# A planned issue order learns of the SBUF port shared by VectorE and GpSimd, and takes its durations from the trace

## The chip, the cores and the metric

The kernel runs on one core of a Trainium2 chip, in one launch. The metric is device time in microseconds (us). The engines are named as the profile names them: PE is the matmul engine (TensorE), PEld its weight loads, DVE is VectorE, ACT is ScalarE, POOL is GpSimd, and SP is the engine whose queue issues every DMA of this kernel. All five take their instructions in program order; one that waits holds up everything behind it on its engine.

## The reference, cut to what matters

The input is 64 sequences of 64 tokens with 256 features, with a context of the same shape. Six pre-norm layers are added one after the other to a residual `x`:

```python
x = x + _L0_attn_ref(_layernorm(x), ...)
x = x + _L0_xattn_ref(_layernorm(x), ctx_2048, ctx_2048)
x = x + _L0_ffn_ref(_layernorm(x), ...)
x = x + _L1_attn_ref(_layernorm(x), ...)
x = x + _L1_xattn_ref(_layernorm(x), ctx_2048, ...)
x = x + _L1_ffn_ref(_layernorm(x), ...)
```

In the kernel they are called a0, x0, f0, a1, x1 and f1. The layer a0 is a causal attention with 16 query heads and 4 key heads of 128, normalised queries and keys and a rotation (RoPE). The layer x0 is an attention over features with 8 heads of 8 tokens each: every head has a 256 by 256 table of scores. The layer f0 is a linear layer plus a routed low-rank expert. The layer a1 is a causal attention with 16 query heads of 16 and one key head. The layer x1 is a cross-attention with 16 heads of 128; only the first 257 context positions are used, which here is the whole context of a sequence. The layer f1 is a gated feed-forward with 704 inner features, whose activations and weights are rounded to 8-bit steps.

## The kernel before

**Tiling.** The 4096 tokens are cut into 16 groups of 256 (`GT`), a residual tile `xt` of 128 partitions by 2 by 256 for each. The first half of the program takes every group through a0, x0, f0 and a1 and stores the residual in DRAM (`mid`); the second half loads it again and does x1 and f1. The halves overlap a little: the first groups of x1 begin while the last groups of the first half run. Set-up work (splitting weights into a high and a low fp16 part, Gram matrices, rounding the f1 weights) is spread between them.

**The planner.** Nothing is emitted where the layer code stands. The layer functions only record operations: `s.o(engine, cost, reads, writes, fn)`, or `s.alt([...], reads, writes)` where two or three engines could do it. `Sched.plan` (L245) then simulates the program greedily with the given costs in ns: at each step it computes for every ready operation the earliest start (ends of what it depends on plus a hand-over time from the table `LATS`, a free buffer, and the time at which its engine is free), sorts the candidates by start, due time and cost, and takes the first that cannot deadlock the buffer pools. `PEN = 400` is added to a DVE candidate that has an alternative. Due times come from `PACE`, `SHIFT` and the table `LEAD` (L1777 on), some 130 offsets by layer and tile. `pe_run` (L225) models PE's clock in windows of `TICK`. `Sched.emit` (L354) calls the recorded functions in the order of the planned starts. The times of the plan are then forgotten: on the chip every engine runs its list in order and waits on semaphores. The only things that the plan decides are the order of each engine's list, the engine of each `alt`, and the assignment of buffers.

**Costs.** `c_act`, `c_acts`, `c_dve`, `c_dve2` and `c_pool` (L363 to L380) give the cost of an operation from its number of elements; many small ones are written as numbers. The plan before knows no dependence between DVE and POOL other than through data.

**Names that the prediction's steps touch.**
- `phl` (L604 to L608, in `softmax_rows`): the normalised probabilities, split into a high part (ACT) and a low part (POOL, or DVE as the alternative). A transposing DMA (`dma_T`, L526) then makes `pt` or `pT`, the input of the PV matmuls (`po` L641, `ctx` L1283, `pc_ps` L1489).
- `xhl` (L540 to L543, in `to_T`): the same split of the normalised residual, then transposed into `xT`. `q1hl` (L1241 to L1244) is the same for a1's queries.
- `ku`, `qu` (L784 to L789, in `rope_bank`): the rotated keys and queries of a0. POOL multiplies (L787), POOL or DVE adds (L788, L789).
- `ln_mv`, `ln_rs`, `xh` (L512 to L521): layer norm. DVE computes statistics, POOL the power, DVE the scaling (`xh` L521).
- `xs_ps` (L990): x0's scores, a pair of matmuls into one PSUM bank, of which DVE takes the row maxima (`xmx` L996). There are 512 pairs. `xt_ps` (L1025): the transposed scores, again 512 pairs, of which ACT takes the exponential (`xpt` L1031). The PSUM pool has 8 banks (`COUNTS`, class B), shared by everything.
- `fam`, `fsc`, `f_w`, `f_b` (L1643 to L1647 and L1619) and `fs` (L1660): the rounding of f1's weights in five chunks on DVE, and the store of the scales to DRAM, one for `w_gu` and one for `w_dn`. It happens at the change-over, when the x0 of the last group is done.
- `acc` of x1 (L387 to L389, by `n_proj`): 48 matmuls for each half of a group's tokens and each block of heads.

Of the kernel before, what the change touches and what calls it, by code (L numbers as in the profile page):

```python
# [13 lines left out]
AF = mybir.ActivationFunctionType  # L14
ALU = mybir.AluOpType
# [6 lines left out]
GT = 256  # L22
# [53 lines left out]
class Sched:  # L76
# [168 lines left out]
    def plan(self):  # L245
        self.clock = [0, 0.0, False]
        free = {e: 0.0 for e in self.ENG}
        slots = {c: [0.0] * n for c, n in self.counts.items()}
# [20 lines left out]
        while ready:  # L269
# [5 lines left out]
            for o in ready:  # L275
                if o.grp > lim and o.grp == int(o.grp):
                    continue
                est = o.tmin
                if o.prev:
                    est = max(est, o.prev[0].start + o.prev[1])  # L280
                for d in o.deps:
                    est = max(est, d.end + LATS[d.eng][o.alts[0][0]])
                need = {}
                for t in o.new:
                    if not t.held:
                        need.setdefault(t.cls, []).append(t)
                ok = True
                for c, n in need.items():
                    fr = slots[c]
                    if len(fr) < len(n):  # L290
                        ok = False
                        break
                    est = max(est, fr[len(n) - 1])
                if not ok:
                    continue
                for e, c, fn in o.alts:
                    st = max(est, free[e])
                    for t in o.new:
                        if t.bank:
                            for e2, u in t.bank.items():  # L300
                                if e2 != e and u + LAT > st:
                                    st = u + LAT
                    cands.append((st, o.due, o.idx, st + c, o, e, fn, need))
                    if st < first[e]:
                        first[e] = st
# [13 lines left out]
            st, _, _, end, o, e, fn, _ = best  # L319
# [42 lines left out]

def c_act(n, ap=0):  # L363
    return 60 + 0.834 * n + 93 * ap


def c_acts(n):
    return 93 + 0.834 * n


def c_dve(n, ap=0):
    return 66 + 1.042 * n + 63 * ap


def c_dve2(n, ap=0):
    return 66 + 0.53 * n + 60 * ap
# [28 lines left out]
def pow2_scale(e, am, exp2, name, root=True):  # L405
# [10 lines left out]
    s.o("PE", 240, [am], [ps], lambda a, p: nc.tensor.matmul(  # L416
# [33 lines left out]
def split_weight(e, src, kc, n, dst, name, prep=None):  # L450
# [30 lines left out]
    for i, w in enumerate(ws):  # L481
# [15 lines left out]
        s.o("DVE", c_dve(pw, 1), [w, sc, hs], [ls], lambda t, a, b0, b, hv=hv, lv=lv:  # L497
# [7 lines left out]
def layer_norm(e, xt, scale=XS):  # L505

    nc, s = e.nc, e.s
    mv = s.T("sm", [128, 2, 2], name="ln_mv")
    st = s.T("sm", [128, 2, 6], name="ln_st")

    for j in range(2):
        s.o("DVE", 336, [xt], [st.sub(j)], lambda x, t, j=j: nc.vector.bn_stats(t[:, j, :], x[:, j, :]))  # L512
    for j in range(2):
        s.o("DVE", 76, [st.sub(j)], [mv.sub(j)], lambda t, m, j=j: nc.vector.bn_aggr(m[:, j, :], t[:, j, :]))
    s.o("DVE", 70, [], [mv], lambda m: nc.vector.tensor_scalar(  # L515
        m[:, :, 1], m[:, :, 1], 1e-5, scale ** -2.0, ALU.add, ALU.mult))
    rs = s.T("sm", [128, 2], name="ln_rs")
    s.o("POOL", 650, [mv], [rs], lambda m, r: nc.gpsimd.tensor_tensor(r, m[:, :, 1], e.mhalf, ALU.pow))  # L518
    xh = s.T("k2", [128, 2, D], name="xh")
    for j in range(2):  # L520
        s.o("DVE", c_dve2(D, 2), [xt, mv, rs], [xh.sub(j)], lambda x, m, r, h, j=j: nc.vector.tensor_scalar(  # L521
            h[:, j, :], x[:, j, :], m[:, j, 0:1], r[:, j:j + 1], ALU.subtract, ALU.mult))
    return xh
# [10 lines left out]
def to_T(e, xh):  # L534
# [8 lines left out]
           ("DVE", c_dve(512), lambda x, _, h: nc.vector.tensor_tensor(h[:, :, 1], x, h[:, :, 0], ALU.subtract))],  # L543
# [26 lines left out]
def softmax_rows(e, s1, scale, fold=False, planes=False):  # L570
# [10 lines left out]
    elif planes:  # L581
        s.o("ACT", 1040, [scale], [s1], lambda a, t: nc.scalar.activation(t, t, AF.Exp, scale=a))
    else:
# [4 lines left out]
        s.o("ACT", 2 * 613, [scale], [s1], f)  # L588
# [7 lines left out]
    s.o("DVE", 165, [], [sm], lambda m: nc.vector.reciprocal(m, m))  # L596
    s.o("DVE", 82, [], [sm], lambda m: nc.vector.tensor_scalar(m, m, 4096.0, None, ALU.mult))
    hls = []
    pl = (lambda t, a: t[:, a]) if planes else (lambda t, a: t[:, :, a])
    for j in range(2):  # L600
# [7 lines left out]
               ("DVE", c_dve(512), lambda t, _, p, h=h: nc.vector.tensor_tensor(pl(p, 1), t[:, h], pl(p, 0), ALU.subtract))],  # L608
# [16 lines left out]
def pv_block(e, phl, vs):  # L625
# [5 lines left out]
    for j in range(2):  # L631
        pt = s.T("k2", [128, 8, 128], F16, name="pt")
        dma_T(e, phl[j], pt, lambda t: t.rearrange("p h a l -> p (h a l)"))
        for hh in range(2):
# [8 lines left out]
            s.o("PE", 4 * 121, vs + [pt], [po], g)  # L643
# [129 lines left out]
def rope_bank(e, ps, tab, dst):  # L773
# [8 lines left out]
    for i in range(2):  # L782
        s.o("ACT", c_act(512), [ps], [sw.sub(i)],
            lambda p, w, i=i: nc.scalar.copy(w[64 * i:64 * i + 64], p[64 - 64 * i:128 - 64 * i]))  # L784
# [3 lines left out]
    s.alt([("DVE", c_dve(512), lambda w, d: nc.vector.tensor_tensor(view(d), view(d), w, ALU.add)),  # L788
# [4 lines left out]
def l0_attn(e, xt):  # L793
    nc, s = e.nc, e.s
    w = e.l0
# [3 lines left out]
    for blk in range(2):  # L799
# [10 lines left out]
        s.o("PE", 480, [sq, w.one], [ss], f)  # L810
# [13 lines left out]
        for c2 in range(4):  # L824
# [3 lines left out]
            if c2 % 2 == 1:  # L828
# [6 lines left out]
                s.o("PE", 500, [sqs[-2], sqs[-1], w.one], [ss], f, duty=0.85)  # L835
# [9 lines left out]
        s.o("PE", 220, [sss], [pst], f)  # L845
# [12 lines left out]
        s.o("PE", 440, [rb], [rk], f)  # L858
# [13 lines left out]
        s.o("PE", 540, [w.tab[0][2], kf], [bps], f, duty=0.79)  # L872
# [4 lines left out]
        for j in range(2):  # L877
# [8 lines left out]
            s.o("PE", 8 * 165, qu + [kf], [sps], f, duty=0.65)  # L886
# [43 lines left out]
def stack_rows(e, src, scale, dst, rows):  # L930
# [4 lines left out]
    if isinstance(scale, float):  # L935
        s.o("ACT", c_act(512), [src], [hl.sub(0)], lambda x, h: nc.scalar.activation(h[:, 0], x, AF.Copy, scale=scale))
        s.o("DVE", c_dve(512), [src, hl.sub(0)], [hl.sub(1)], lambda x, h0, h: nc.vector.scalar_tensor_tensor(
            h[:, 1], x, scale, h[:, 0], ALU.mult, ALU.subtract))
    else:
        s.o("ACT", c_act(512, 1), [src, scale], [hl.sub(0)],  # L940
            lambda x, a, h: nc.scalar.activation(h[:, 0], x, AF.Identity, scale=a))
        s.o("DVE", c_dve(512), [src, scale, hl.sub(0)], [hl.sub(1)], lambda x, a, h0, h: nc.vector.scalar_tensor_tensor(
# [11 lines left out]
def l0_xattn(e, xt, g, I):  # L954
# [24 lines left out]
    for j in range(2):  # L979
        mx = s.T("sm", [128, 4, 4, 2], name="xmx")  # L980
        sp = [None, SPACE[0]]
        for bs in range(4 * j, 4 * j + 4):
            for v in range(2):
                for h in range(2):
# [8 lines left out]
                    s.o("PE", 230, rows(v) + [K.sub((u, r)) for u in range(2) for r in range(3)], [ps], f, duty=0.46)  # L993
# [5 lines left out]
        s.o("PE", 110, [mx], [mps], lambda m, p: nc.tensor.transpose(p, m.rearrange("p a b c -> p (a b c)"), e.ident))  # L999
# [11 lines left out]
    for j in range(2):  # L1011
        y = s.T("k1", [128, 2, 2, 2, 4, 8], name="y")
        for b in range(2):
            po = s.T("B", [128, 2, D], name="xo_ps")
            for hs in range(2):
                bs = (2 * j + b) * 2 + hs
                pt = [s.T("k2", [128, 2, D], name="xpt") for _ in range(4)]
                for v in range(2):
                    for h in range(2):
# [8 lines left out]
                        s.o("PE", 230, rows(v) + [Q[v].sub((v, 3, j)), K], [ps], f, duty=0.46)  # L1028
# [23 lines left out]
            s.o("PE", 440, [so], [pt_], f)  # L1052
# [3 lines left out]
            s.o("DVE", 170, [pt_], [rc], lambda p, r: nc.vector.reciprocal(r, v4(p)[:, :, :, 8]))  # L1056
# [5 lines left out]
            s.o("DVE", 270, [pt_, rc], [y.sub(b)], f)  # L1062
# [5 lines left out]
        s.o("PE", 220, [y], [yo], f)  # L1068
# [19 lines left out]
def l0_ffn(e, xt):  # L1088
# [6 lines left out]
    for j in range(2):  # L1095
# [23 lines left out]
        s.o("PE", 110, [hm], [pt], lambda h, p: nc.tensor.transpose(p, h.rearrange("p a r -> p (a r)"), e.ident))  # L1119
# [3 lines left out]
        s.o("PE", 470, [hT, w.bw], [po], lambda h, b, p: nc.tensor.matmul(p, h, b, start=True, stop=True))  # L1123
# [63 lines left out]
def l1_attn(e, xt):  # L1187
# [25 lines left out]
    s.o("DVE", c_dve(GT, 1), [k1, w.hl, kh], [K],  # L1213
# [11 lines left out]
    s.o("ACT", 4 * 90, [ps], [v1], f)  # L1225
# [5 lines left out]
    s.o("DVE", 720, [v1, w.m2], [vbd], f)  # L1231
# [11 lines left out]
    s.alt([("DVE", c_dve(512), lambda x, h0, h: nc.vector.tensor_tensor(h[:, 1], x, h[:, 0], ALU.subtract)),  # L1243
# [14 lines left out]
    for j in range(2):  # L1258
# [28 lines left out]
        s.o("PE", 690, [vbd] + pTs, [cps.sub(j)], f, duty=0.46)  # L1287
# [17 lines left out]
def gram_setup(e, I, name):  # L1305
# [42 lines left out]
    s.o("DVE", c_dve(514), [g, sc, w.w.sub(0)], [w.w.sub(1)],  # L1348
# [5 lines left out]
def value_out_setup(e, I):  # L1354
# [28 lines left out]
    for b in range(4):  # L1383
        u = pieces(s, 8, 256, f"x1wn{b}")
        d = s.fixed(e.dx.tile([128, 2, 2048], F16, tag=f"wdn{b}", name="wd"))
        for i in range(4):
# [9 lines left out]
            s.o("DVE", c_dve(512, 1), [t, sc, hl.sub(0)], [hl.sub(1)], lambda t, a, h0, h:  # L1396
# [117 lines left out]
def rms_gram(e, g, T, x, xs=1.0):  # L1514
# [3 lines left out]
    for j in range(2):  # L1518
# [14 lines left out]
        s.o("DVE", 75, [ps], [ac], lambda p, ac: V.tensor_tensor(ac, ac, p[:, 256:257], ALU.add))  # L1533
# [3 lines left out]
    s.o("POOL", 740, [ms], [rs], lambda m, r: nc.gpsimd.tensor_tensor(r, m, e.mhalf, ALU.pow))  # L1537
# [3 lines left out]
def l1_xattn(e, xt, g, I):  # L1541
# [8 lines left out]
    s.o("DVE", c_dve(512, 1), [ctx, e.ctx_sc, chl.sub(0)], [chl.sub(1)], lambda x, a, _, t:  # L1550
# [16 lines left out]
    s.o("DVE", 330, [w.bo, rk], [L], f)  # L1567
# [5 lines left out]
    s.o("PE", 430, [L, w.i2], [rps], f)  # L1573
# [6 lines left out]
    for blk in range(2):  # L1580
        es = s.T("sm", [128, 2], name="x1esc")
        s.o("DVE", 130, [rq, w.exps[blk]], [es], lambda r, a, t: nc.vector.tensor_scalar(t, r, a, None, ALU.mult))
        k = [s.T("k2", [128, 2, GT], name="k8") for _ in range(4)]
        q = [s.T("k2", [128, 2, GT], name="q8") for _ in range(4)]
        for (dst, nm, T, bias) in ((k, "ki", cTs, w.kb), (q, "q", xT, w.qb)):
            for c2 in range(4):
# [10 lines left out]
                s.alt([("DVE", c_dve(512), f1), ("ACT", 716, f2)], [ps, bias], [dst[c2]])  # L1597
        s1 = s.T("k4", [128, 16, S], name="s1")
        for j in range(2):
# [9 lines left out]
            s.o("PE", 8 * 165, q + k, [sps], f, duty=0.65)  # L1609
# [59 lines left out]
def l1_ffn(e, xt):  # L1669
# [9 lines left out]
    s.o("DVE", 70, [am], [sx], lambda am, sx: V.tensor_scalar(sx, am, 1.0 / 127, 1e-8, ALU.mult, ALU.max))  # L1679
    s.o("DVE", 75, [sx], [ix], lambda sx, ix: V.reciprocal(ix, sx))  # L1680
# [8 lines left out]
    for j in range(2):  # L1689

        gu = [s.T("k4", [128, 2, HI], name="gu") for _ in range(2)]
        for a in range(4):
# [18 lines left out]
        s.o("DVE", c_dve(704), [gu[0]], [sig], lambda g, t: V.scalar_tensor_tensor(t, t, 1.0, g, ALU.add, ALU.mult))  # L1711
        s.o("DVE", c_dve(704), [sig], [ah.sub(j)], lambda t, ah, c=c: V.tensor_reduce(
            ah[:, c], t, AX.XY, ALU.max, apply_absolute_value=True))
        s.o("DVE", 75, [sx], [s2.sub(j)], lambda x, s2, c=c: V.tensor_tensor(s2[:, c], x[:, c], x[:, c], ALU.mult))
        s.chain("DVE", [
            (75, lambda s2, ah, sh, ih, c=c: V.tensor_tensor(ah[:, c], ah[:, c], s2[:, c], ALU.mult)),
            (75, lambda s2, ah, sh, ih, c=c: V.tensor_scalar(sh[:, c], ah[:, c], 1.0 / 127, 1e-8, ALU.mult, ALU.max)),
            (75, lambda s2, ah, sh, ih, c=c: V.reciprocal(ih[:, c], sh[:, c])),  # L1718
            (75, lambda s2, ah, sh, ih, c=c: V.tensor_tensor(ih[:, c], ih[:, c], s2[:, c], ALU.mult))],
# [13 lines left out]
        s.o("PE", 6 * 117, [hT, w.dn], [po], f)  # L1733
# [231 lines left out]
```

## Time and profile before

| | us |
|---|---|
| median of 3 runs | 2777.41 (2777.24 to 2780.94) |
| the profiled execution | 2781.26 |
| its span (first to last instruction) | 2779.5 |
| PE busy | 2460.3 |
| DVE busy | 2139.8 |
| ACT busy | 1521.3 |
| POOL busy | 1499.2 |
| granted TensorE clock, mean | 0.942 |

PE has over 24,000 matmuls. Its busy time contains stretches at the lower clock, in which a matmul takes twice as long. The span is longer than PE's busy time by 319 us. DVE's busy time includes what an instruction waits inside the engine once it has begun: the same operation on the same shape can have very different durations in the trace. Bytes are few (82 GB/s on average).

### The profile page before, as it was taken

Reading aid. Unit: us, or ns where it says so; the run is one execution under the profiler, and the core shown is the slowest. Engines: PE = TensorE matmul, PEld = TensorE weight load, DVE = VectorE, ACT = ScalarE, POOL = GpSimd, SP = SyncE. Lnnn points to the kernel's source line nnn. Section 1 sums busy time; section 2 is a strip of 40 time slices with the busy share of each in tenths; the row PEclk is TensorE's granted clock in tenths of the full one; section 3 lists DMA queues with packets and bytes.
Section 4 is the critical chain, followed back from the end, with each engine's and each line's share of the span. In section 5 each row is a group of like instructions: output and inputs, shape, how many; then the busy total and the mean of one; then the engine's idle time right before and its main releaser. Section 6 shows DMA issues by size and latency. Waiting matters only on the chain.

```text
span 2779.5 us, 61709 instructions
## 1 busy us (share of the span) xinstructions
PE 2460.3 (89%) x24136; PEld 1718.9 (62%) x24136; DVE 2139.8 (77%) x4827; ACT 1521.3 (55%) x2878; POOL 1499.2 (54%) x1258
## 2 busy tenths in 40 slices
PE   4889988989889989999899899579999999999995
PEld 3656565545565655565465556357777778877773
DVE  8886887898888879789888776637776767767765
ACT  6755637557568656666674466244544444444441
POOL 5895556686776768668767344223333333333321
PEclk9989999989999999999999999789999999999997
DMA  6333235345445345423345543413223232222211
GB/s 187 77 73 68 47 78 128 97 109 124 92 128 145 91 100 113 113 62 75 76 86 119 139 81 68 73 34 61 53 51 62 58 64 52 53 51 53 58 31 33
DMA packets 488532, 226.55 MB, mean 82 GB/s; under 512 B 341808, under 2 KB 463792, under 8 KB 488240
## 3 DMA queue, kind: packets, MB, share of 16 engines
q1 hardware_dynamic: 488240, 222.60, 35.5%
q8 instruction: 190, 3.11, 0.5%
q14 instruction: 102, 0.84, 0.1%
HBM read 87.98 MB, written 33.56 MB: 44 GB/s over the span
## 4 chain that ended last, share of the span: by engine, by line
PE 55%; DVE 18%; DMA 7%; ACT 4%; POOL 4%; issue 3%; SPq 1%; POOLq 0%; DVEq 0%; ACTq 0%
PE acc L387 4%; PE acc L389 4%; PE acc L388 4%; PE qk_ps L387 4%; PE xt_ps L1025 4%; PE qk_ps L389 4%; PE qk_ps L388 4%; DVE xmx L996 4%; PE pc_ps L1489 3%; PE xo_ps L1039 3%; PE xs_ps L990 2%; PE s_ps L1607 2%; DMA xT<-xhl 2%; PE s_ps L885 1%; DMA pt<-phl 1%
## 5 line engine op out<-in xcount | busy, mean ns | idle before, releaser
L1031 ACT ACTIVATE xpt<-xt_ps,xes 128x512 f32<-128x512 f32 x512 | 341.2, 689 | 113.8 <-PE xt_ps L1025 104.3
L996 DVE TENSOR_REDUCE xmx<-xs_ps 128x2 f32<-128x512 f32 x512 | 330.4, 681 | 38.1 <-PE xs_ps L990 34.5
L578 POOL TENSOR_TENSOR s<-s,sm_mx 128x1024 f32<-128x1024 f32 x96 | 184.6, 1924 | 254.0 <-DVE sm_mx L577 240.9
L389 PE MATMUL acc<-x1wn,pc 128*128 128x256 f16 x1024 | 280.9, 274 | 2.9 <-DVE pc L1495 2.9
L387 PE MATMUL acc<-x1wn,pc 128*128 128x256 f16 x1024 | 280.9, 274 | 0.5 <-ACT pc L1493 0.4
L388 PE MATMUL acc<-x1wn,pc 128*128 128x256 f16 x1024 | 280.8, 274 | 0.0
L604 POOL TENSOR_TENSOR s<-s,sm_sm 128x512 f32<-128x512 f32 x192 | 207.0, 1096 | 127.0 <-DVE f1ih L1718 73.0
L518 POOL TENSOR_TENSOR ln_rs<-ln_mv,mhalf 128x2 f32<-128x2 f32 x96 | 69.7, 726 | 340.0 <-DVE ln_mv L515 318.2
L1025 PE MATMUL xt_ps<-ovl 64*128 64x256 f16 x1024 | 197.2, 276 | 14.1 <-DMA ovl<-mneg 5.7
L990 PE MATMUL xs_ps<-ovl 64*128 64x256 f16 x1024 | 167.4, 294 | 45.8 <-DVE xmx L996 33.0
L1495 DVE SCALAR_TENSOR_TENSOR pc<-pc_ps,pc 128x512 f16<-128x512 f32 x256 | 162.8, 679 | 42.8 <-ACT pc L1493 42.3
L1596 ACT ACTIVATE q<-qk_ps,x1qb 128x256 f32<-128x256 f32 x250 | 104.8, 470 | 150.9 <-PE qk_ps L389 145.0
L607 POOL TENSOR_TENSOR phl<-s,phl 128x512 f16<-128x512 f32 x139 | 169.5, 1229 | 29.4 <-ACT phl L606 29.1
L784 ACT COPY sw<-q_ps 64x512 f32<-64x512 f32 x256 | 148.3, 580 | 61.3 <-PE q_ps L389 48.3
L787 POOL TENSOR_TENSOR sw<-sw,rp0s 128x512 f32<-128x512 f32 x128 | 167.6, 1320 | 15.1 <-ACT sq L785 14.9
L606 ACT CAST phl<-s 128x512 f16<-128x512 f32 x192 | 115.8, 618 | 104.1 <-POOL s L604 100.6
L1596 ACT ACTIVATE k<-qk_ps,x1kb 128x256 f32<-128x256 f32 x250 | 104.5, 470 | 108.8 <-PE qk_ps L389 87.5
L1493 ACT ACTIVATE pc<-pc_ps 128x512 f16<-128x512 f32 x256 | 131.6, 623 | 43.0 <-PE pc_ps L1489 42.7
L990 PEld LDWEIGHTS <-ovl 64*128 64x128 f16 x1024 | 64.9, 97 | 141.7 <-issue 126.5
L387 PE MATMUL q_ps<-xT,l0w 128*128 128x256 f16 x512 | 144.9, 283 | 6.6 <-DVE xmx L996 2.4
L789 POOL TENSOR_TENSOR qu<-qu,sw 128x512 f32<-128x512 f32 x116 | 148.3, 1286 | 3.9 <-DVE nr_t L562 2.8
L387 PE MATMUL qk_ps<-cTs,x1wki 128*128 128x256 f16 x512 | 142.6, 278 | 5.8 <-DVE pc L1495 4.0
(424 smaller groups left out, 7671.4 us busy)
## 6 DMA issues: line engine op xcount, KB each, us to landing
ovl<-hl_d SPq DMA_DIRECT2D x192, 64.0 KB
vx<-vt SPq DMA_DIRECT2D x64, 128.0 KB
ctx<-in_ctx_dram SPq DMA_DIRECT2D x32, 256.0 KB
hl_d<-hl SPq DMA_DIRECT2D x64, 128.0 KB
q1st<-q_d SPq DMA_DIRECT2D x128, 64.0 KB
wd<-w_hl SPq DMA_DIRECT2D x32, 256.0 KB
cst<-chl SPq DMA_DIRECT2D x64, 128.0 KB
xt<-in_x_dram SPq DMA_DIRECT2D x16, 256.0 KB
```

The costliest lines, as they stand in the source:

```text
L387: nc.tensor.matmul(out, lh, rh, start=(st and i == 0), stop=False, **kw)
L388: nc.tensor.matmul(out, lh, rl, start=False, stop=False, **kw)
L389: nc.tensor.matmul(out, ll, rh, start=False, stop=(i == n - 1), **kw)
L578: s.o("POOL", 1900, [mx], [s1], lambda m, t: nc.gpsimd.tensor_tensor(t, t, bc(m, 2, 64), ALU.subtract))
L604: s.o("POOL", 1030, [sm], [s1.sub(j)], lambda m, t, h=h: nc.gpsimd.tensor_tensor(t[:, h], t[:, h], bc(m[:, h], 2, 64), ALU.mult))
L607: s.alt([("POOL", c_pool(482), lambda t, _, p, h=h: nc.gpsimd.tensor_tensor(pl(p, 1), t[:, h], pl(p, 0), ALU.subtract)), ("DVE", c_dve(512 ...
L787: s.o("POOL", 1225, [sg], [sw], lambda t, w: nc.gpsimd.tensor_tensor(v(w), v(w), bc(t, 1, 8), ALU.mult))
L990: nc.tensor.matmul(a[-1][:, mc, :], q0[hh, bs, 128 * mc:128 * mc + 128], k[hh, bs, :], start=True, stop=True)
L996: nc.vector.tensor_reduce(m[:, 2 * v + h, bs % 4, :], p, AX.X, ALU.max))
L1025: nc.tensor.matmul(p[:, n, :], k[hh, bs, 128 * n:128 * n + 128], q[hh, bs, :], start=True, stop=True)
L1031: nc.scalar.activation(t, p, AF.Exp, scale=a))
L1596: nc.scalar.activation(d[:, c, :], p[:, c, :], AF.Identity, bias=b[:, b0 + c:b0 + c + 1])
```

## The change

`plan` keeps, beside the time at which each engine is free, a time for the port on DVE's side and one on POOL's side. Every POOL operation counts as using the port; a DVE operation does if its cost is of the new type `Port`, a float with a name. A POOL operation starts in the plan no earlier than the end of the last Port operation on DVE, and a Port operation on DVE no earlier than the end of the last POOL operation. The other changes are numbers: costs are set anew, most of them higher, few lower (`ctx` on PE from 690 to 510, the score matmuls from 165 to 150 each). `c_dve2`, and the new `c_dves` that replaces `c_dve` where both inputs lie in SBUF, return a `Port`. `LEAD`, `PACE`, `SHIFT`, `PEN`, `LATS` and all recorded functions stay as they are. The diff, cut to its core; the left-out lines are of the same kinds:

```diff
@@ plan
         free = {e: 0.0 for e in self.ENG}
+        port = dict(DVE=0.0, POOL=0.0)
...
                 for e, c, fn in o.alts:
                     st = max(est, free[e])
+                    if e == "POOL":
+                        st = max(st, port["DVE"])
+                    elif isinstance(c, Port):
+                        st = max(st, port["POOL"])
...
-            st, _, _, end, o, e, fn, _ = best
+            st, _, _, end, o, e, fn, _, lock = best
+            if lock or e == "POOL":
+                port[e] = end
             if e == "PE":
                 end = self.pe_run(st, end - st, o.duty)
...
+class Port(float):
+    pass
+
 def c_act(n, ap=0):
-    return 60 + 0.834 * n + 93 * ap
+    return 88 + 0.834 * n + 100 * ap
 def c_acts(n):
-    return 93 + 0.834 * n
+    return 148 + 0.834 * n
 def c_dve(n, ap=0):
-    return 66 + 1.042 * n + 63 * ap
+    return 72 + 1.042 * n + 63 * ap
+def c_dves(n, ap=0):
+    return Port(c_dve(n, ap))
 def c_dve2(n, ap=0):
-    return 66 + 0.53 * n + 60 * ap
+    return Port(66 + 0.53 * n + 60 * ap)
...
@@ layer_norm
-    s.o("DVE", 70, [], [mv], lambda m: nc.vector.tensor_scalar(
+    s.o("DVE", Port(130), [], [mv], lambda m: nc.vector.tensor_scalar(
...
-    s.o("POOL", 650, [mv], [rs], lambda m, r: nc.gpsimd.tensor_tensor(r, m[:, :, 1], e.mhalf, ALU.pow))
+    s.o("POOL", 705, [mv], [rs], lambda m, r: nc.gpsimd.tensor_tensor(r, m[:, :, 1], e.mhalf, ALU.pow))
@@ to_T
-           ("DVE", c_dve(512), lambda x, _, h: nc.vector.tensor_tensor(h[:, :, 1], x, h[:, :, 0], ALU.subtract))],
+           ("DVE", c_dves(512), lambda x, _, h: nc.vector.tensor_tensor(h[:, :, 1], x, h[:, :, 0], ALU.subtract))],
@@ softmax_rows
-    s.o("DVE", 165, [], [sm], lambda m: nc.vector.reciprocal(m, m))
-    s.o("DVE", 82, [], [sm], lambda m: nc.vector.tensor_scalar(m, m, 4096.0, None, ALU.mult))
+    s.o("DVE", Port(205), [], [sm], lambda m: nc.vector.reciprocal(m, m))
+    s.o("DVE", Port(130), [], [sm], lambda m: nc.vector.tensor_scalar(m, m, 4096.0, None, ALU.mult))
...
-               ("DVE", c_dve(512), lambda t, _, p, h=h: nc.vector.tensor_tensor(pl(p, 1), t[:, h], pl(p, 0), ALU.subtract))],
+               ("DVE", c_dves(512), lambda t, _, p, h=h: nc.vector.tensor_tensor(pl(p, 1), t[:, h], pl(p, 0), ALU.subtract))],
@@ rope_bank
-    s.alt([("DVE", c_dve(512), lambda w, d: nc.vector.tensor_tensor(view(d), view(d), w, ALU.add)),
+    s.alt([("DVE", c_dves(512), lambda w, d: nc.vector.tensor_tensor(view(d), view(d), w, ALU.add)),
            ("POOL", 1225, lambda w, d: nc.gpsimd.tensor_tensor(view(d), view(d), w, ALU.add))], [sw], [dt])
@@ l0_xattn
-                    s.o("PE", 230, rows(v) + [K.sub((u, r)) for u in range(2) for r in range(3)], [ps], f, duty=0.46)
+                    s.o("PE", 290, rows(v) + [K.sub((u, r)) for u in range(2) for r in range(3)], [ps], f, duty=0.46)
...
-                        s.o("PE", 230, rows(v) + [Q[v].sub((v, 3, j)), K], [ps], f, duty=0.46)
+                        s.o("PE", 290, rows(v) + [Q[v].sub((v, 3, j)), K], [ps], f, duty=0.46)
@@ l1_attn
-        s.o("PE", 690, [vbd] + pTs, [cps.sub(j)], f, duty=0.46)
+        s.o("PE", 510, [vbd] + pTs, [cps.sub(j)], f, duty=0.46)
@@ l1_ffn
-        s.o("PE", 6 * 117, [hT, w.dn], [po], f)
+        s.o("PE", 850, [hT, w.dn], [po], f)
```

## The prediction, made before the changed kernel ran

> **What bounds the kernel now.** I read the page's busy times first, then a table by stage, then TensorE's waits, then the timeline at its worst places. The page:
>
> ```profile
> span 2779.5 us, 61709 instructions
> PE 2460.3 (89%) x24136; PEld 1718.9 (62%) x24136; DVE 2139.8 (77%) x4827; ACT 1521.3 (55%) x2878; POOL 1499.2 (54%) x1258
> PE   4889988989889989999899899579999999999995
> PEclk9989999989999999999999999789999999999997
> ```
>
> PE is busy 89% of the span, and the idle rest is not spread evenly. By stage (start-up; the sixteen groups' first half; the change-over to the second half; the second half; the end):
>
> ```profile
> 0.00:200.00 200.00, 141.65 (x1235) 98.49 (x1236) 168.51 (x402) 123.20 (x231) 157.23 (x144) 0.89 0.41 112
> 200.00:1740.00 1540.00, 1398.95 (x14023) 882.71 (x14021) 1263.05 (x2819) 962.56 (x1738) 1012.71 (x835) 0.95 0.42 97
> 1740.00:1840.00 100.00, 46.87 (x369) 31.06 (x368) 53.71 (x113) 25.84 (x57) 30.64 (x26) 0.68 0.38 73
> 1840.00:2720.00 880.00, 843.69 (x8340) 688.35 (x8338) 627.08 (x1438) 400.68 (x839) 288.18 (x245) 0.99 0.26 52
> 2720.00:2780.00 60.00, 29.12 (x178) 18.32 (x176) 27.47 (x58) 9.00 (x14) 10.47 (x11) 0.73 0.13 27
> ```
>
> The columns are PE, PEld, DVE, ACT, POOL, then clock and DMA. PE idles 58, 141, 53, 36 and 31 us in them. Only in the first three can an issue order win or lose much; there DVE is the next fullest engine (82% from 200 to 1740). What PE waits for between 200 and 1740:
>
> ```profile
> PE xs_ps L990 <- DVE xmx L996: 30.0, 26, 6.4
> PE q_ps L387 <- DMA xT<-xhl: 9.9, 7, 2.5
> PE ctx L1283 <- DMA pT<-phl: 7.9, 8, 2.0
> ...
> PE xt_ps L1025 <- ACT xpt L1031: 3.8, 8, 0.9
> ```
>
> With its smaller rows this list gives DVE about 54 us, the transposing DMAs (xT, pT, pt) 27, the rest to ACT and other DMAs. The largest row has a picture, DVE's line first:
>
> ```profile
> 184.45 10.83 DVE L996 TENSOR_REDUCE xmx<-xs_ps 128x2 f32<-128x512 f32 x16
> 185.18 1.18 PE L990 MATMUL xs_ps<-ovl 64*128 64x256 f16 x4 [0.30 <-DVE xmx L996]
> ...
> 195.67 1.96 PE L1322 MATMUL g_ps<-g_w 128*128 128x257 f32 x4
> ```
>
> Here the order has twenty xs_ps pairs almost on end. Each needs one DVE maximum of 0.68 us (10.83/16), PE needs 0.22 (two matmuls 0.11 apart in the chain of waits), so PE steps at DVE's pace, and the granted clock from 185 to 200 is 0.50 to 0.52.
>
> **The change, part by part.** It changes no arithmetic. The planner's costs go up, DVE operations marked Port and all POOL operations exclude each other in the plan, and so the emitted order and the choice among alternatives change. I laid the two built programs' instruction lists side by side.
>
> 1. *Work that leaves DVE.* 89 two-input operations go from DVE to POOL: 53 phl, 20 xhl, 15 ku/qu, 1 q1hl. Their rows:
>
> ```profile
> L608 DVE TENSOR_TENSOR phl<-s,phl x53: 674/1359/2860, 119.1 to 2725.5; 128x512 f16<-128x512 f32 x53
> L607 POOL TENSOR_TENSOR phl<-s,phl x139: 1145/1157/1697, 171.5 to 2727.2; 128x512 f16<-128x512 f32 x139
> ```
>
> (min/median/max ns.) A spread from 674 to 2860 for one shape is what waiting for a shared resource looks like; POOL's own instruction hardly varies. By the busy time of lines 608, 543 and 788 in each stretch, DVE loses 16 us of the first 200, 53 us of the next 1540, and some 40 after 1740. The last 40 are hidden: from 1840 PE is busy 96% and TensorE's order there is the same in both lists but for a few us. For the 53, the floor is the share of DVE time that PE feels, 54/1263, so 2 us; the ceiling is all 53. DVE holds 54 of PE's 141 idle us, 38%, and 38% of 53 is 20: I take **-20**.
>
> A table of the Trainium skill speaks against the move: GPSIMD Engine Reference, section 4.1, puts elementwise work on VectorE, GPSIMD being about twice as slow with two inputs. The minimum agrees (1145 to 674), the median does not (1157 to 1359). By the rule the 89 moves cost 42 us of engine time (89 x 0.47), by the medians they save 18.
>
> 2. *What POOL gets.* Between 200 and 1740, 32 phl, 6 xhl and 8 ku/qu: 38 x 1.16 + 8 x 1.29 = 54 us on top of 1013. They stand in the chains that end in those transposes. POOL's idle time falls by a tenth (527 to 473); 27 us of waits longer by a tenth are 3, and 54 times those waits' share of PE's idle time (27/141) is 10. I take **+5**. In the first 200 us POOL is busy 157 and gets 17 more, DVE 16 fewer; ends -8 (half of DVE's) and +17, taken 0.
>
> 3. *Bunching.* Runs of xs_ps pairs with no more than 0.9 us of other matmuls between them: before, four of eight or more (20, 12, 9, 8; 49 pairs); after, eight (20, 16, 10, 9 and four of 8; 87 pairs), the 20 right after the 10 and before eleven xt_ps. xt_ps pairs, whose exponential on ACT takes 0.689 us, come in runs of five or more 8 times before (42 pairs) and 19 times after (110). Beyond the first four of a run, which the eight PSUM banks can hold, each pair costs 0.68 - 0.22 = 0.46 us: xs_ps (55 - 33) x 0.46 = 10; xt_ps, at 0.47, (34 - 10) x 0.47 = 11: **+21**. If the banks hold only two, it is 14 + 22 = 36; if the work squeezed out runs elsewhere in the room the bunches leave, 0.
>
> 4. *The clock.* After the run at 185 the matmuls go at half rate until about 202, some 7 us of work taking 3.5 longer. Before has two runs of ten or more, after three and the eleven xt_ps. I take **+5**, ends 0 and 14 (four more runs of eight, 3.5 each). The Trainium skill (TensorE: Matmul & The Clock Gate, What's actually happening) throttles after an idle window of about 3.4 us; the row shows half rate while matmuls ran in every such window. By the rule this term would be 0.
>
> 5. *Change-over.* Before, DVE stalls on a small store, and two such stores lie 16 us apart:
>
> ```profile
> 1756.32 0.37 SPq L1660 DMA_DIRECT2D fs<-fsc  x1
> 1772.45 0.37 SPq L1660 DMA_DIRECT2D fs<-fsc  x1
> ...
> 1767.53 0.89 DVE L1643 TENSOR_REDUCE fam<-f_w 128x1 f32<-128x704 f32 x1 [6.12 <-DMA fs<-fsc]
> ```
>
> After, all five weight chunks (L1643 to L1647) stand together on DVE, the stores follow each other on SP with one chunk between, and the 6.1 us wait mostly goes. But 96 acc matmuls (10.5 us at 0.11), which run before q1 of the last group now and cover DVE's stretch, stand behind that group's o1_ps afterwards. Behind the first store's new waiter on DVE, the last group's router (L1112), sit hm and that group's residual adds. Net 10.5 - 6.1 = **+4**; ends -6 (only the wait) and +10.5.
>
> The other raised costs (ACT, small DVE, PE) change no instruction; their effect is the order counted above.
>
> Sum: -20 + 5 + 0 + 21 + 5 + 4 = +15 on the profiled execution's 2781.3 us (span 2779.5 and 1.8 around it), 2796. The median, 2777.4, lies 3.9 lower, so **2792**.
>
> **Rivals.**
> - *Relief of DVE decides* (faster). Term 1 at its ceiling, -53, others as taken: 2777 - 53 + 35 = 2759; with no bunching cost 2738. For it: DVE is the fullest engine behind PE and the largest row of waits is its. Against: that row comes from pairs in runs, which POOL's help does not shorten. It decides once waits for DVE fall by more than 35 us.
> - *POOL becomes late.* +17 at start-up, +10 in term 2, the bunches at 36 and the rest as taken: 2777 - 20 + 17 + 10 + 36 + 5 + 4 = 2829. For: POOL is 79% busy in the first 200 us. Against: 66% later.
> - *Nothing net.* The lock is only in the plan, on the chip the engines start when they may: L521 (mean 640 ns, minimum 314) stays as it is, and relief of some 35 cancels the rest: 2777.
>
> **How the numbers follow.** Forecast, 2784 to 2815: 0.46. POOL late, above: 0.14. Nothing net, within 0.2% (2772 to 2783, about what a measurement here can tell from no change): 0.09. Relief, below 2772: 0.31. So slower 0.60, same 0.09, faster 0.31. The range, 2748 to 2840, goes into both outer cases until about 0.1 is left out at each side; the forecast's own is 2784 to 2815.
>
> **What would show it.** Term 1: lines 608 and 543 gone from DVE, DVE under 1215 us in the first half's stretch. Terms 3 and 4: waits of L990 on L996 above 30 us, those of L1025 on L1031 well above 3.8, the clock below 0.95 there. Term 5: no wait of 6 us for the store, and o1_ps of the last group followed by 96 acc matmuls. Wrong if L990's waits fall, or if the second half, which I count as unchanged, differs by over 10 us.

## The result, and the profile after

After takes 2792.5 us (median of 20 executions, 2781.4 to 2799.2) against 2778.5 for before in the same sessions: ratio 1.0044, 95% interval [1.0031, 1.0056]. It is slower by 0.44%. The profiled execution took 2795.1 us. The page of after:

```profile
span 2793.3 us, 61820 instructions
PE 2444.7 (88%) x24136; PEld 1721.3 (62%) x24136; DVE 1957.6 (70%) x4728; ACT 1535.5 (55%) x2900; POOL 1579.8 (57%) x1340
PE   3779998877998989899999889449999999999995
PEclk9799999968999999899999899769999999999997
```

DVE is busy 182 us less than before and POOL 81 more, yet the span is longer. (The moved operations are only part of the 182: e3 and e4 below show the moves alone and the order alone.) The PE digits show two places: a weaker start (3779 for 4889) and a deeper hole at the change-over (two slices of 4 where before has a 5 and a 7). By stage (PE, PEld, DVE, ACT, POOL, then clock, DMA):

```profile
0.00:200.00 200.00, 123.14 (x1080) 89.63 (x1080) 142.71 (x352) 108.80 (x204) 150.78 (x140) 0.85 0.41 113
200.00:1740.00 1540.00, 1386.61 (x13852) 881.77 (x13850) 1166.85 (x2762) 972.99 (x1750) 1053.12 (x879) 0.94 0.39 95
1740.00:1840.00 100.00, 40.43 (x458) 26.50 (x455) 52.94 (x120) 32.29 (x63) 34.93 (x31) 0.67 0.29 66
1840.00:2720.00 880.00, 854.07 (x8488) 696.44 (x8488) 553.31 (x1406) 409.16 (x867) 324.37 (x277) 0.98 0.28 55
```

In the first 200 us TensorE does 155 matmuls fewer than before (1080 for 1235). From 1840 on it is busy 854 us where it was 844, although the last group's a1 still runs into it here (its last o1_ps starts at 1857). What TensorE waits for from 200 to 1740:

```profile
PE n_ps L1387 <- DMA n_o<-in_x_o_dram: 17.1, 1, 17.1
PE ctx L1299 <- DMA pT<-phl: 14.9, 11, 6.3
PE xs_ps L1006 <- DVE xmx L1012: 14.6, 28, 2.0
PE q_ps L403 <- DMA xT<-xhl: 13.7, 6, 8.1
PE f_ps L403 <- DMA xT<-xhl: 10.0, 8, 2.5
...
PE xt_ps L1041 <- ACT xpt L1047: 1.6, 3, 0.7
```

(us in total, times, longest. Lines of after stand 16 below those of before.) The row that the prediction expected to grow, xs_ps on xmx, has halved, 30.0 to 14.6; the one on xpt fell from 3.8 to 1.6. The rows that end in a transposing DMA fed by POOL have grown: ctx 7.9 to 14.9, q_ps 9.9 to 13.7, f_ps 3.6 to 10.0. A load that came late stops TensorE once for 17.1 us; e4 below, which has after's order of loads and matmuls, has this wait too (16.6), and no other plan has more than 1.1 us of it.

To see where the 14 us arise, time has to be compared at equal work, not at equal time, because the order of the work differs. I count every matmul by the median time from one of its shape to the next (2034 us of work in all) and read off when a given sum of work is reached. "Start-up" is the first 100 us of work, the "first half" goes to 1100, the "change-over" to 1300, the "second half" is the rest to the last matmul. Each row is one profiled execution:

```
                   start-up  first half  change-over  second half     against before
before                193.4      1461.5        293.3        826.4
after                 210.1      1475.6        306.5        796.3     +16.7  +14.0  +13.2  -30.1
```

So after loses 44 us by the end of the change-over and wins 30 back behind it, in the part of the program that the prediction counted as unchanged.

### The profile page after: what moved, and what is told of

Read it like the earlier page. It is cut to its first block, busy times and chain, and to the rows that moved or that the text cites. A ratio compares the mean times of both kernels' runs of the same rounds, so it can differ in the third digit from the quotient of the medians.

```text
span 2793.3 us, 61820 instructions
## 1 busy us (share of the span) xinstructions
PE 2444.7 (88%) x24136; PEld 1721.3 (62%) x24136; DVE 1957.6 (70%) x4728; ACT 1535.5 (55%) x2900; POOL 1579.8 (57%) x1340
## 4 chain that ended last, share of the span: by engine, by line
PE 53%; DVE 17%; DMA 11%; POOL 8%; ACT 5%; issue 5%; SPq 1%; POOLq 0%; DVEq 0%; ACTq 0%
PE acc L403 5%; PE acc L405 5%; PE acc L404 5%; DVE xmx L1012 4%; PE xt_ps L1041 3%; PE qk_ps L403 3%; PE qk_ps L404 3%; PE qk_ps L405 3%; PE xo_ps L1055 3%; PE pc_ps L1505 3%; DMA xT<-xhl 3%; DMA pT<-phl 2%; DMA pt<-phl 2%; POOL phl L623 2%; PE s_ps L901 1%
## 5 line engine op out<-in xcount | busy, mean ns | idle before, releaser
L594 POOL TENSOR_TENSOR s<-s,sm_mx 128x1024 f32<-128x1024 f32 x96 | 192.8, 2010 | 219.4 <-DVE sm_mx L593 217.4
L620 POOL TENSOR_TENSOR s<-s,sm_sm 128x512 f32<-128x512 f32 x192 | 200.0, 1058 | 133.6 <-DVE sm_sm L613 79.6
L623 POOL TENSOR_TENSOR phl<-s,phl 128x512 f16<-128x512 f32 x192 | 222.2, 1169 | 25.3 <-ACT phl L622 22.2
L1041 PE MATMUL xt_ps<-ovl 64*128 64x256 f16 x1024 | 180.0, 283 | 9.1 <-DMA ovl<-mneg 5.3
L1006 PE MATMUL xs_ps<-ovl 64*128 64x256 f16 x1024 | 160.0, 292 | 26.6 <-DVE xmx L1012 14.6
L805 POOL TENSOR_TENSOR qu<-qu,sw 128x512 f32<-128x512 f32 x128 | 162.6, 1279 | 4.5 <-DVE qu L802 1.4
L1055 PE MATMUL xo_ps<-xpt,xve 128*32 128x256 f32 x2048 | 156.5, 395 | 4.2 <-ACT xpt L1047 4.0
L403 PE MATMUL q_ps<-xT,l0w 128*128 128x256 f16 x512 | 142.6, 279 | 6.4 <-ACT sss L855 2.7
L405 PE MATMUL q_ps<-xT,l0w 128*128 128x256 f16 x512 | 142.2, 278 | 2.1 <-DVE l0w L514 2.1
```

Source lines behind the costliest of these rows:

```text
L403: nc.tensor.matmul(out, lh, rh, start=(st and i == 0), stop=False, **kw)
L405: nc.tensor.matmul(out, ll, rh, start=False, stop=(i == n - 1), **kw)
L594: s.o("POOL", 1900, [mx], [s1], lambda m, t: nc.gpsimd.tensor_tensor(t, t, bc(m, 2, 64), ALU.subtract))
L620: s.o("POOL", 1030, [sm], [s1.sub(j)], lambda m, t, h=h: nc.gpsimd.tensor_tensor(t[:, h], t[:, h], bc(m[:, h], 2, 64), ALU.mult))
L623: s.alt([("POOL", c_pool(482), lambda t, _, p, h=h: nc.gpsimd.tensor_tensor(pl(p, 1), t[:, h], pl(p, 0), ALU.subtract)), ("DVE", c_dves(51 ...
L1041: nc.tensor.matmul(p[:, n, :], k[hh, bs, 128 * n:128 * n + 128], q[hh, bs, :], start=True, stop=True)
```

## The experiments

Both sets of costs can stand in one file. Nine of the twelve kernels are built so, with three switches: `NEW_NUM` (the plan goes by the durations of after), `NEW_PORT` (the port rule holds), `NEW_DUE` (due times are worked out from the durations of after). With all of them on the plan is that of after, with all off that of before. In these nine the lines stand 40 below those of before (xs_ps L1030, f1o_ps L1772).

### The two parts, and the moved operations

**e1_port**, the rule alone.

```diff
 def NEW_NUM(o, t):
-    return True
+    return False
 def NEW_PORT(o, t):
     return True
-NEW_DUE = True
+NEW_DUE = False
```

Expected: 

> The port rule alone: the plan excludes Port operations on DVE and POOL operations from each other, but goes by the durations and due times of before. In this plan all 192 phl are on POOL (before 139), as after. Theory A (what leaves DVE is worth some 27 us in the second half; a changed order costs at start-up, in the middle of the first half and at the change-over): between 2750 and 2800, TensorE's waits for hqT in the second half fall from 33 us to below 20. Theory B (the relief is worth nothing; only how the order happens to fall counts): anywhere from 2770 to 2810, with the waits for hqT still near 33.

Measured: 2756.2 us, ratio 0.9920 [0.9899, 0.9942]: faster than before by 0.8%. The waits for hqT fell to 13.5 us, as theory A said; e3 and e4 show that its reason, the operations that leave DVE, does not hold.

**e2_num**, the durations alone: `NEW_NUM` and `NEW_DUE` on, `NEW_PORT` off.

Expected: 

> The new durations alone, no port rule in the plan. 33 phl stay on DVE (before 53, after 0). Theory A: the gain of the second half is mostly missing (waits for hqT above 25 us), the cost of a changed order is paid, so 2785 to 2815, not below after (2792.5). Theory B: 2770 to 2810, no relation to the number of phl on DVE.

Measured: 2815.0 us, 1.0128 [1.0103, 1.0152]. With these two the change seems taken apart: -22 for the rule, +36 for the durations, and their sum is the +14 of after. The runs with another tie setting, below, show how little that says.

**e3_move**, the order of before, the 89 operations on POOL.

```diff
         order.sort(key=lambda o: (o.start, o.grp, o.idx))
+        for o in order:
+            if o.eng == "DVE" and (o.W or o.R)[0].parent.name in ("phl", "xhl", "ku", "qu", "q1hl"):
+                o.fn = next((fn for e, _, fn in o.alts if e == "POOL"), o.fn)
         return order
```

Expected: 

> The order of before to the last instruction on TensorE, ACT and the DMA queue, with the same 89 operations (53 phl, 20 xhl, 15 ku and qu, 1 q1hl) given to POOL at the place where DVE had them. This is terms 1 and 2 of the prediction alone. As predicted: -20 + 5 + 0, so 2764. Theory A: the second half gains some 27 us, the first between 0 and 20, POOL's start-up may lose a few: 2730 to 2760. Theory B (the gain of the second half comes from the new order of DVE's list): 2773 to 2790. The rival that POOL becomes late: above 2785, in the first 200 us most of all.

Measured: 2800.0 us, 1.0081 [1.0056, 1.0105]. Moving the 89 operations, with nothing else, costs 21 us. Two rows of its waits, over the whole span:

```profile
PE f1o_ps L1735 <- DMA hqT<-hq: 32.7, 15, 8.6
PE xs_ps L993 <- DVE xmx L999: 30.0, 31, 7.0
```

Before has 34.0 and 33.0 there. DVE is busy 90 us less (2050.1 for 2139.8) and the waits for its maxima fell by 3 us; the second half gained nothing (831.1 us for 826.4). Theory A expected a gain and theory B at most 2790; by its range the rival that POOL becomes late is the one that holds, though not "in the first 200 us most of all": start-up +7.7, first half +9.5, second half +4.8. Between 200 and 1740 the waits for the transposing DMAs rise only from 26.9 to 32.8 us. The operations stand in POOL's list where the plan had put them for DVE, so this is the price of the bare move, not of every plan that gives them to POOL.

**e4_back**, the order of after, the same 89 operations (`BACK` holds their numbers) back on DVE.

```diff
         order.sort(key=lambda o: (o.start, o.grp, o.idx))
+        for o in order:
+            if o.idx in BACK:
+                o.fn = next(fn for e, _, fn in o.alts if e == "DVE")
         return order
```

Expected: 

> The order of after, with the same 89 operations given back to DVE. Theory A: loses what the relief brought, 2792 + 20 to 40, so 2812 to 2832, TensorE's waits for hqT in the second half back at 30 us. Theory B: 2787 to 2800. The rival that POOL is late: below 2785.

Measured: 2797.8 us, 1.0066 [1.0045, 1.0087], an interval that overlaps that of after. This is theory B's range; the waits for hqT are 19.4 us, not the 30 of theory A. By stage 207.0, 1479.8, 306.4 and 794.5 us, nearly those of after (210.1, 1475.6, 306.5, 796.3). In after's order it hardly matters which engine does the 89 operations, and the gain of the second half is there with them on DVE. How long DVE is busy there does not decide it either: from 1900 to 2700 it is busy 535.9 us here and 536.8 us in e3, which gains nothing. What the change does, it does through the order.

The order also changes what these operations take on DVE. The same 53 phl subtractions as in the prediction's first row, here (least, median and most ns):

```profile
L627 DVE TENSOR_TENSOR phl<-s,phl x53: 673/684/2165, 103.4 to 2741.1; 128x512 f16<-128x512 f32 x53
```

In before's order the median is 1359. Over the whole program DVE is busy 2010.1 us here for 2139.8 in before, with the same operations on it. So in after's order the operations on DVE wait far less once they have begun, and the whole is not faster for it.

### The same four plans with a setting that means nothing

If a gain or loss comes from what a rule says, it should survive a change of the planner that has no meaning on the chip. `EPS` says by how many ns two candidates may differ and still count as tied.

```diff
-EPS = 50
+EPS = 60
```

Expected, for before, for the port rule alone, for the durations alone, and for after:

> Before, with one setting of the planner changed that has no meaning on the chip: candidates within 60 ns of the earliest start count as equal, not within 50 (EPS). Theory S (the times differ because the two parts of the change do something): within 10 us of before, 2768 to 2788. Theory L (any other order of this greedy plan scatters by some 20 us, and the -22 of the port rule and the +36 of the durations are two draws): between 2750 and 2820, more than 10 us away from before.

> The port rule alone (durations of before), with the same tie setting of 60 ns. Theory S: 2746 to 2766, as with 50. Theory L: between 2740 and 2810, and as likely above before as below.

> The new durations alone, with the same tie setting of 60 ns. Theory S: 2805 to 2825. Theory L: between 2760 and 2820.

> After, with the same tie setting of 60 ns. Theory S: 2782 to 2802. Theory L: between 2750 and 2820; together with the other three the effect of the port rule and of the durations changes its size by more than 15 us or its sign.

Measured (us, and the ratio to before with its interval):

| plan | ties within 50 ns | ties within 60 ns |
|---|---|---|
| before | 2778.5 | 2794.2, 1.0046 [1.0018, 1.0073] |
| port rule alone | 2756.2, 0.9920 [0.9899, 0.9942] | 2798.9, 1.0067 [1.0046, 1.0089] |
| durations alone | 2815.0, 1.0128 [1.0103, 1.0152] | 2785.8, 1.0026 [1.0002, 1.0050] |
| both (after) | 2792.5, 1.0044 [1.0031, 1.0056] | 2762.7, 0.9943 [0.9917, 0.9968] |

With the other setting the change is a gain of 31.5 us (2794.2 to 2762.7) where it was a loss of 14, the port rule alone is +5 where it was -22, and the durations alone -8 where they were +36. Ten nanoseconds in a tie rule move single plans by 16 to 43 us. Theory L holds: the total of any one of these plans says more about the luck of its order than about its rule, and neither e1 nor e2 shows what its part is worth.

By stage the same runs do show something:

```
                   start-up  first half  change-over  second half     against before
port rule from the start
  after                210.1      1475.6        306.5        796.3     +16.7  +14.0  +13.2  -30.1
  e1_port              204.0      1481.1        253.4        805.5     +10.6  +19.6  -39.9  -20.8
  c2_port_tie60        209.0      1484.4        294.5        803.3     +15.6  +22.9   +1.2  -23.1
  c4_after_tie60       209.1      1469.3        282.2        796.3     +15.7   +7.8  -11.0  -30.0
no port rule
  e2_num               182.5      1481.4        317.0        832.4     -10.9  +19.9  +23.7   +6.1
  c1_before_tie60      190.4      1456.4        313.7        826.8      -3.0   -5.1  +20.4   +0.4
  c3_num_tie60         186.2      1450.2        307.0        833.6      -7.2  -11.4  +13.7   +7.2
```

Two columns go with the rule in every plan: the start-up is 11 to 17 us longer than before, the second half 21 to 30 us shorter. The change-over goes with nothing: 253 to 317 us. (In e1, the shortest, 718 matmuls follow the last yo of x0 up to the last o1_ps of a1, in before 313.)

Most of the second half's gain stands in TensorE's waits between 1900 and 2700, 30.2 us in all in before and 4.6 in after. Before:

```profile
PE f1o_ps L1732 <- DMA hqT<-hq: 20.9, 12, 3.1
PE qk_ps L387 <- DVE pc L1495: 4.0, 7, 0.7
```

After:

```profile
PE pc_ps L1505 <- DMA pt<-phl: 2.2, 5, 0.7
PE f1o_ps L1748 <- DMA hqT<-hq: 1.8, 3, 1.0
```

The row on hqT is 20.9 to 23.8 us in the four plans of the table without the rule (before among them) and at most 2.6 in the four with it. hqT is the transposed input of f1's second matmul. Between `gu_ps` and it lies f1's chain through DVE, ACT and POOL (L1700 to L1724), full of Port operations. In the plan of before, f1o_ps starts 14.3 us behind gu_ps; with the rule these operations wait for POOL in the plan, and it is 18.7 (16.2 with the durations too, 11.5 with the durations alone). (This is the first of a group's two tiles, the one that waits.) So TensorE's order has 198 other matmuls in between with the rule alone, or 178 with the durations too, instead of 168 (124 with the durations alone): in before f1o_ps starts 14.8 to 16.8 us behind gu_ps, some 2 us of wait included; in after 15.8 to 16.9 with next to none. Whether this distance is the cause is tried in h4 below.

### The rule only where it gains

**h1_port_late.** The order is that of before until behind the change-over (on the chip, until 1942 us).

```diff
 def NEW_PORT(o, t):
-    return True
+    return t >= 1700e3
```

(`NEW_NUM` and `NEW_DUE` off.) Expected: 

> Before, with the port rule only from 1700 us of planned time on; the order is that of before to the last instruction until behind the change-over. Theory P (the port rule makes the second half some 25 us faster, because its plan puts f1o_ps later behind gu_ps, 18.7 us where the plan of before has 14.3 and the chip needs about 16.5; its costs lie in the start-up and the first half): 2748 to 2760, TensorE's waits for hqT below 20 us. Theory L (the second half of the other runs differs by chance of the order): 2770 to 2786.

Measured: 2753.5 us, 0.9925 [0.9901, 0.9949]. Its second half takes 805.9 us, 20.5 less than before's, the other stages are within 6 us of before's (its profiled execution took 2765.1 us, 12 above its median). Its waits from 1900 to 2700 are 17.2 us in all, among them:

```profile
PE pc_ps L1529 <- DMA pt<-phl: 8.3, 14, 2.0
...
PE f1o_ps L1772 <- DMA hqT<-hq: 2.0, 1, 2.0
```

This is the one gain of the change that was forecast and then found, in size and in place: the rule in the second half's plan brings it. The cause that theory P names, the distance of f1o_ps, is another matter, as the next run shows.

**h4_hqt_2500**, one number of before.

```diff
-def dma_T(e, src, dst, flat):
+def dma_T(e, src, dst, flat, more=0):
...
-    s.o("SP", DMA_NS + 700, [src], [dst], lambda t, p: nc.sync.dma_start(
+    s.o("SP", DMA_NS + 700 + more, [src], [dst], lambda t, p: nc.sync.dma_start(
...
-        dma_T(e, hq, hT, lambda t: t)
+        dma_T(e, hq, hT, lambda t: t, 2500)
```

Expected: 

> Before, with one number changed: the plan takes the transposing DMA of hq to hqT to be 2500 ns longer, so f1o_ps is planned 16.5 us behind gu_ps, not 14.3. No port rule, no other duration; the order until the change-over is that of before. Theory P: most of the gain of the second half, 2753 to 2765, waits for hqT below 22 us (before 34). If the second half of the port plans is faster through something else (where DVE and POOL avoid each other), 2772 to 2784 with the waits for hqT falling all the same.

Measured: 2771.0 us, 0.9987 [0.9968, 1.0006]: no difference that can be told. The row on hqT is gone from 1900 to 2700, as both expected, but this stands in its place:

```profile
PE pc_ps L1489 <- DMA pt<-phl: 22.6, 14, 2.5
```

It was 2.1 in before. f1o_ps moved behind other work (184 matmuls behind gu_ps, more than the 178 of after), and x1's own chain, phl to pt, now comes late by as much. So the distance of f1o_ps alone does not bring the gain. In the plans with the rule neither chain waits long (2.2 and 1.8 us in after); a likely reason is that the rule lets the plan know that f1's chain on DVE and x1's softmax on POOL delay each other. That is argued, not shown: which of the rule's many moves brings the two chains into step was not tried.

**h2_late_hold**, h1 with the fourth group of the second half held back.

```diff
         for g in range(ng):
             s.grp = ng + g
+            s.tmin = {3: 1550e3}.get(g, 0.0)
             group(g, 1, sb)
```

Expected: 

> As the port rule from 1700 us on, and the fourth group of the second half is held back in the plan until 1550 us, so that 46 us of matmuls stand between the last yo of x0 and the last o1_ps of a1 in TensorE's order, where before has 26.6 and the port rule alone has 66.7. Theory F (the change-over costs what it has too few matmuls to cover): 17 to 20 us below the port rule from 1700 us on, so 2730 to 2743, and TensorE idle some 40 us between those two, not 61. Rival (what is held back is missing earlier, where it covered waits of the first half): within 5 us of the port rule from 1700 us on.

Measured: 2762.9 us, 0.9954 [0.9937, 0.9972], 9 us above h1. TensorE has 44.5 us of work between the last yo and the last o1_ps (before 24.9) and idles 46.2 us there instead of 61.0, as theory F says; but behind it more is left to do: at 1300 us of work the gain is used up (change-over 296.2 us for 293.3). Neither range is met: the gain of theory F did not come, and the time lies beyond the 5 us of the rival, whose reason fits best. Covering the hole with work taken from elsewhere is no gain by itself.

**h6_both_late**, h1 with the durations too.

```diff
 def NEW_NUM(o, t):
-    return False
+    return t >= 1750e3
```

Expected: 

> As the port rule from 1700 us of planned time on, and from 1750 us on the new durations too (due times as before); the order until behind the change-over is that of before. In the runs so far TensorE waited 34 to 36 us behind 1900 us where port rule and durations were both in (after, its tie of 60, its order with the operations given back), 45 to 46 where the port rule was alone, 60 to 68 without it. If the durations do that: 2740 to 2750, waits of some 35 us behind 1900. If not, or if the second half of after is faster through what it had left to do at the change-over: within 4 us of the port rule from 1700 on, 2749 to 2758.

Measured: 2756.2 us, 0.9920 [0.9896, 0.9944], the same as h1; TensorE waits 45.1 us behind 1900 where h1 waits 45.0. The durations add nothing that can be told to h1. The two are the fastest versions together with e1, and all three beat both kernels; unlike e1 they owe it to a stage whose gain was there in every plan with the rule.

## Why the prediction was right, and where it was not

The forecast, 2792, met 2792.5, and the likeliest outcome came. Its reasons did not: two of the conditions under which it called itself wrong came true (the waits of xs_ps on xmx fell, and the second half differs by 30 us). Errors of both signs cancelled: by stage the sum had 0, +11, +4 and 0, the chip +16.7, +14.0, +13.2 and -30.1.

1. *Work that leaves DVE, -20.* DVE is busy 1166.9 us from 200 to 1740, below the 1215 named; this fall of 96 us is more than the 53 of the moved operations, because those that stay take less time too (1194.6 us in e4, with the moved ones back). The price was wrong in sign. The step took DVE's share of TensorE's waits as the share of the relief that TensorE feels. e3 took 90 us of DVE's busy time away in before's own order, and the waits for xmx fell by 3. The rule that was weighed there (the Trainium skill, GPSIMD Engine Reference, section 4.1) had the sign in before's order: it made the moves 42 us dearer in engine time, and e3 lost 21. In after's order, e4 shows no such loss by the move. The median that spoke against the page, 1359 ns, belongs to before's order: in e4's it is 684 on DVE, to 1158 on POOL.
2. *What POOL gets, +5 and 0.* The waits for xT, pT and pt between 200 and 1740 rose from 27 to 50 us, but not for the reason given, POOL's added work: they are 32.8 us in e3, which adds that work to before's order, and 46.8 in e4, which takes it out of after's. They are over 46 us in three of the four plans with the rule from the start (33.4 in the fourth, c4) and at most 27 in the four without. At start-up the end of +17 that I set aside met the 16.7 that came, and that is luck: with the operations back on DVE, e4 still loses 13.6 there, and e3 loses 7.7. What came:

```profile
PE v_ps L403 <- DMA xT<-xhl: 17.7, 3, 8.7
...
PE bias_ps L887 <- POOL kf L879: 7.0, 4, 2.9
...
PE s_ps L901 <- POOL qu L805: 3.6, 1, 3.6
```

These are waits of the first 200 us of after; the first was 1.4 in before, all those for POOL together 0.2. Every plan with the rule from the start has them. The likely reason is that few groups are in flight there, so that nothing covers an operation that the plan delays on POOL; this was not tried.
3. *Bunching, +21.* This step fell. Over the whole span, counted as in the prediction, the xs_ps pairs in runs of eight or more and the waits of xs_ps on xmx are 49 and 33.0 us in before, 87 and 14.6 in after, 65 and 10.0 in e1, 16 and 16.4 in e2. There is no order in that. xt_ps has 110 pairs in long runs for 42 and waits 1.6 us for 3.8. The count itself is soft: with every matmul in between taken at its median time to the next one in the trace, the pairs in runs of eight or more are 125 in before and 120 in after. One stretch (184 to 195 us of before) was read as the rule for all runs. What the waits go with is the order and not DVE's load: they are 30.0 us in e3 (before's order, the operations moved) and 16.6 in e4 (after's order, the operations back). What in the order does it, perhaps what else stands in DVE's list in front of the maxima, is not shown.
4. *The clock, +5.* From 200 to 1740 it fell from 0.95 to 0.94, as forecast, and its longest stretch at half rate lies where xs_ps pairs wait for xmx, as the term says (PE, PEld, DVE, ACT, POOL, then clock, DMA):

```profile
559.00:596.00 37.00, 25.07 (x148) 10.51 (x147) 28.52 (x53) 19.43 (x35) 18.95 (x17) 0.50 0.36 90
```

It also falls where TensorE waits for something else (0.51 from 675 to 692, mostly in the wait for the late load; start-up 0.89 to 0.85). No run takes the clock's price apart from that of the waits, so the +5 stays open.
5. *Change-over, +4.* The events came as named. All five chunks stand together on DVE, and what the last group needs of DVE stands behind them:

```profile
1767.58 1.20 DVE L1659 TENSOR_REDUCE fam<-f_w 128x4 f32<-128x1024 f32 x1
...
1782.76 0.95 DVE L1659 TENSOR_REDUCE fam<-f_w 128x3 f32<-128x768 f32 x1
...
1789.72 0.23 DVE L1128 TENSOR_SCALAR lg<-f_ps,m 128x8 f32<-128x8 f32 x1 [1.84 <-DMA fs<-fsc]
```

The router's product f_ps was ready at 1772. TensorE's next matmul waits 14.9 us for an operation on DVE (s) that stands behind the chunks, and a later one 13.5 us for the last group's xT:

```profile
1787.46 0.29 PE L1671 MATMUL fw_ps<-identb,f_b 128*128 128x128 bf16 x1 [14.91 <-DVE s L1626]
...
1808.84 0.39 PE L403 MATMUL q_ps<-xT,a1w 128*128 128x256 f16 x1 [13.47 <-DMA xT<-xhl]
```

The term was mis-sized, 13.2 for 4: the work that lost its cover was priced by the cover (10.5 us of acc), not by the chain that now lies bare, from the last yo to the last o1_ps 98.2 us long for 86.0, with 249 matmuls in it for 313. And the waits for the store did not go: 1.8 and 3.4 us of them fall on others.
6. *The second half, 0.* "Busy 96%" and "TensorE's order there is the same but for a few us" were both read rightly, and both hid the point: the 4% were mostly waits that a small change of order could end (30.2 us from 1900 to 2700, 4.6 in after). f1o_ps moving 10 matmuls down is one of the moves, but h4 shows that it is not enough alone.

The forecast's chances (0.60 slower) were of the right kind, but for a reason it didn't name: the other orders of this plan that were run lie from 25 us below before to 37 above.

## What to carry to other kernels

When a planner decides the order, every edit of a cost draws a new order; before a gain or a loss is put down to what the edit means, change something that means nothing and see how far the time moves (here 16 to 43 us, more than the effect). Compare such kernels at equal work and stage by stage: where all variants with a rule fall on one side in a stage, the rule does something there, and applying it in that stage alone is the test (2753.5 us, in the forecast range). A long row of waits is no price: in h4 the 20.9 us behind hqT went away and 22.6 us came up behind the next chain.

## What was not expected of the hardware

- Executions of one kernel differ by up to 1.2% (before 2767.9 to 2800.4 in the session of the tie runs, 2763.7 to 2786.0 in that of h1). Four profiles whose instruction order is the same up to the change-over (before, h1, h4, h6) agree there within 2 us at start-up and 1.5 at the change-over, but spread from 1452 to 1467 us over the first half. So how much of the +14 in after's first half is real can't be told from its profile alone; the 17.1 us of the late load come again in e4.
- An order planned with the rule shortens what DVE's instructions take, although the chip never sees the plan's times: the 53 phl go from a median of 1359 ns to 684 (before and e4). It does not end the long cases: xh took 314, 411 and 2581 ns (least, median, most) in before and 321, 409 and 2454 in after, its mean fell from 640 to 543.
